# A masked-adjacency layer on one core: the bias as one row, the weight matrix on the loads' queue, two blocks of edge weights moved from ScalarE to VectorE

## The chip, the cores and the metric

The kernel runs on one core of a Trainium2 chip, as one launch. Its time is device microseconds for the launch, and a kernel's time is the median of its runs. The profiled execution is one more run, whose engines and DMA queues were recorded; its span runs from the first to the last recorded instruction of the program and is a little shorter than its device time.

## The reference

The inputs are `x` (4096 x 64), `adj` (4096 x 4096, f32, zeros and ones), a 64 x 64 weight and a bias of 64.

```python
h = jnp.maximum(_layernorm(x, axis=-1), 0.0)
support = h @ weight
mask = (adj != 0).astype(support.dtype)
rank = jnp.cumsum(mask, axis=1)
deg = rank[:, -1:]
k = jnp.minimum(deg, 100.0)
pos = rank - (deg - k)
w = mask * jnp.where(pos > 0, 0.5 ** (k - pos), 0.0)
out = x + w @ support + bias
```

So each row of `adj` gives an edge at a set column the weight one half to the power of the number of set columns behind it, and columns with a hundred or more set ones behind them get nothing. The 64 MB of `adj` are read once; everything else is small.

## The kernel before

The rows are cut into 32 tiles of 128, and each tile is a 2 MB read. The task `load(n)` brings a tile in one transfer, or tiles 0, 1, 28 and 29 in two and tiles 30 and 31 in three. Four tile buffers (`NA`) go round: a load waits until the tile four before it has been read out of its buffer.

A tile then goes through a line of tasks, each on one engine. `convert` (VectorE, L544) turns the f32 tile into mask bytes, four of the eight column pieces per instruction. `flip` (VectorE, L554) transposes it in 32 x 32 blocks. `totals` (TensorE, L562), `split` (ScalarE, L570) and `suffix` (TensorE, L583) count the set columns behind each place. `clamp` (VectorE, L589) limits the count, with a small correction `excess`. `place` (TensorE, L599 and L603) writes exponents into four PSUM banks, j = 0 to 3. `weigh(n, j, part)` (ScalarE, L617) takes one bank through the exponential and writes a block of weights in `wk`; `PARTS` names tiles whose blocks are cut into several instructions. `aggregate(u, h)` (TensorE, L637) multiplies the weights of a pair of tiles with `hr`, the support. After each group of four tiles, `drain` adds the bias (ScalarE L650 or VectorE L652), `turn_back` (TensorE, L658) and `finish` (VectorE, L664) bring the result into row order and add `x`, and `store` writes it.

Ahead of this stands the setup. `fetch` (L339) brings `x` in two halves; `turn`, `center`, `square`, `spread` on TensorE and ScalarE make the layer norm. `support(n)` (TensorE, L512, four groups) multiplies the result with `w2`, which holds the weight matrix twice on its diagonal blocks. `scale(n)` (VectorE, L515) applies the norm's root, and `first` (ScalarE, L522) and `second` (VectorE, L525) split the support into the two parts of `hr`. The correction `excess` comes from `count` (TensorE, L529) and `counted` (VectorE, L532). `warm` (L467) puts spare matmuls on TensorE where the plan sees it idle.

The order on each engine is laid down when the program is built: `plan` takes the tasks one after the other, by their needs, by assumed durations and by the tuned due times in `DUE`, and the engines run them in that order. SyncE issues the loads, the fetches, `load_rest` and the stores in the planned order on one queue. Before, the weight's two transfers are issued by ScalarE on its own queue, at L360, ahead of everything else there. `load_rest` brings the bias into `bias_sb`, one value to a partition (64 elements of 4 bytes in two transfers, L347).

There is a way of making a block of weights on VectorE in the code, which no tile uses: for a pair (tile, j) in `QUICK`, `encode` (L624) turns the exponents into the bits of a float and `take` (L628) scales them into `wk`, in place of `weigh`.

Of the kernel before, what the change touches and what calls it, by code (L numbers as in the profile page):

```python
# [8 lines left out]
F32 = mybir.dt.float32  # L9
# [8 lines left out]
ALU = mybir.AluOpType  # L18
# [18 lines left out]
PIECES = LOADS  # L37
UNITS = [(t, h0, h1) for t in TILES for h0, h1 in (HALVES if t in HALF_UNITS else ((0, 8),))]

PARTS = {31: ((0, 4), (4, 6), (6, 8))}  # L40
QUICK = set()
DRAINS = [(g, 0, 4, g < 6) for g in range(7)] + [(7, 0, 2, False), (7, 2, 4, True)]
STORES = [(0, 0, 16), (1, 0, 12), (1, 12, 14), (1, 14, 16)]
NA, NM, NT, NW, NV, NB = 4, 4, 4, 2, 5, 2

DUE = {
    "fetch": [-6573, -7310],
    "load": [-5992, -6683, -5596, -6079, -7169, -9667, -9541, -11493, -10919, -11290, -11530, -11235, -10266, -10315,
    -11211, -10957, -10678, -11366, -12321, -13820, -14131, -14798, -15615, -14819, -13978, -13919, -13846, -13027,
    -13593, -14902, -7667, -6694, -6587, -6826, -7245, -7519, -6878, -3159, 1510, 1620],  # L50
    "load_rest": [-344],
    "constants": [-454, 600],
    "order_of": [-456],
    "stack": [-625],
    "turn": [-172, 214, 16, 393, 528, 858, 499, 332],
    "turned": [1435, 859, 693, 1141, 1083, 537, 293, 544],
    "center": [171, -98, -659, -200],
    "square": [465, 438, 248, 1102],
    "relu": [1137, 791, 1387, 1058],
    "spread": [-15, 13, -661, -370],  # L60
    "support": [21, -60, -416, -201],
    "scale": [-210, 55, -42, 94],
    "root": [1695],
    "power": [262],
    "count": [530],
    "counted": [543],
    "first": [-860, -667, 302, 408],
    "second": [-75, 111, -482, -354],
    "convert": [-384, -581, 457, 322, -121, -884, 963, 534, -34, -1077, 787, 1056, 108, -349, 764, 1004, 101, -704, 979,
    1309, 707, -163, 1369, 1105, 584, 389, 925, 815, 565, 524, 1124, 802, 750, 45, 1343, 901, 420, 492, 1332, 749, 610,  # L70
    333, 1547, 1282, 1005, 482, 1549, 1648, 364, 550, 1413, 1518, 264, 195, -2196, 1220, 1067, 223, 2066, 2141, -755,
    469, 1297, 60, 1670, 2032],
    "flip": [-564, -432, -860, -830, -320, -589, 240, -276, 665, 258, -130, -71, -67, 442, -190, 483, 174, 848, 950,
    856, 1062, 326, 1060, 1245, 1617, 444, 1652, 901, 1412, 474, 1484, 1416, 1678, 1523, 1720, 1723, 1966, 1776, 2138,
    1090],
    "totals": [615, 533, 701, 950, 1159, 658, 942, 1158, 1268, 370, 1091, 793, 1042, 571, 1431, 749, 1321, -201, 952,
    -123, 771, 524, 719, 698, 807, 1068, 901, 954, 1308, 1166, -194, 861],
    "split": [645, -612, 977, 535, 538, 291, 747, 660, 1196, 965, 1319, 1075, 778, 1018, 734, 1262, 1360, 1594, 1519,
    1656, 1385, 1551, 1729, 1073, 1530, 1511, 1247, 1740, 1524, 2582, -853, -74],
    "suffix": [446, -15, -61, -786, 763, -236, 795, -313, 93, -188, 459, 552, 669, 835, 216, 631, 395, 564, 584, 950,  # L80
    672, 1258, 1076, 1183, 627, 1332, 531, 1082, 731, 1768, 1451, 1290],
    "clamp": [90, 357, 63, 429, -223, 517, 200, 1181, 126, 1287, 489, 1021, 423, 1392, 1268, 1349, 1153, 1062, 714,
    1190, 873, 1239, 869, 899, 504, 1578, -309, -1871, 1035, -1395, 1481, 1978],
    "place": [-1043, -999, -185, 32, -515, -449, -256, -109, -246, 699, -474, 58, -329, -577, -226, 20, -85, 232, -531,
    862, 244, 461, 334, 493, 422, 197, -375, -4620, -3255, -4102, -4101, -13758],
    "weigh": [124, 602, 275, 1009, 635, 1298, 1060, 979, 251, 1028, 726, 1335, 205, 1247, 1050, 936, 591, 779, 700,
    1681, 194, 1357, 1572, 1538, 896, 884, 250, 1348, 553, 1355, 731, 1523, 431, 1605, 947, 1785, 604, 1354, 180, 929,
    381, 2058, 362, 1907, 1129, 801, 383, 1150, 582, 2063, 1301, 2112, 752, 1610, 506, 1510, 659, 2136, 1339, 1936,
    1101, 1819, 669, 1804, 1010, 1979, 967, 1974, 1005, 1542, 510, 2083, 822, 1632, 648, 2361, 1289, 2144, 1196, 1898,
    733, 2030, 647, 2806, 833, 2056, 893, 1515, 249, 1745, 1172, 2639, 1558, 1904, 878, 2400, 992, 2310, 857, 2878,  # L90
    2393, 2725, 1566, 1672, 772, 2619, 1366, 3218, -1655, 2443, -1184, 2580, -535, 2589, 1767, 2743, 78, 2081, 468,
    2913, -3989, 2783, -4899, 2547, -5001, 3060, 2146, -4693, 1918, 2884, 1281, 2811, 2340, 2930, 1917, 2959],
    "aggregate": [334, -267, 593, 289, 1191, 1307, 964, 874, 634, -145, 1348, -270, 752, 1012, -6, 1122, 727, 337, 806,
    -760, 1172, 1394, 515, 867, 914, 74, 936, -373, 1753, 2069, 346, 1555, 388, -82, 1324, 248, 1341, 843, 1279, 1957,
    864, 854, 630, 886, 1416, 1688, 1445, 1564, 1277, 701, 781, 607, 1776, 1685, 1033, 1943, 1694, 873, 660, 1016, 1406,
    1009, 1086, 2299, 1563, 543, 1077, 1566, 1268, 1601, 1408, 2689, 1367, 1074, 1372, 1672, 1796, 1257, 1627, 2498,
    1552, 1370, 1423, 1005, 2226, 1650, 1563, 1956, 2147, 1545, 1525, 1823, 1923, 1908, 2041, 2335, 1453, 1178, 1529,
    2289, 2123, 1291, 1467, 2761, 1965, 1183, 2006, 1763, 2046, 1812, 1619, 2707, 2251, 1680, 1492, 2718, 1786, 1494,
    1802, 3130, -4938, 2631, 2110, 3528, 12, 1317, 1118, -4615],
    "drain": [66, -394, 53, 500, 1525, 818, 356, 1592, -14523],  # L100
    "turn_back": [225, 460, 1136, 1049, 1175, 2364, 545, 1770, -12563],
    "finish": [564, 45, 886, 1501, 2162, 1424, 2379, 1937, -13193],
    "store": [2230, 2470, 2247, -14086],
}
WAIT = 250, 60, 150, 60, 0
PE, DVE, ACT, POOL, SP = range(5)
# [7 lines left out]
def last_of(n, j):  # L114

    return ("encode", n, j) if (n, j) in QUICK else ("weigh", n, j, len(PARTS.get(n, (0,))) - 1)


def tasks():
# [4 lines left out]
    def task(f, args, engine, due, hold, lag, needs, pool=None):  # L124
        if f in DUE:
            due = DUE[f][sum(k[0] == f for k in found)] / 10
        found[f, *args] = f, args, engine, due, hold, lag, needs, pool
# [3 lines left out]
        task("fetch", (r,), SP, 0.5, 0, 0, [])  # L131
    for n, (t, _, _) in enumerate(LOADS):
        task("load", (n,), SP, n, 0, 0, [("convert", m, i) for m, (pt, h0, h1) in enumerate(PIECES) if pt == t - NA for i in range((h1 - h0 + 3) // 4)])
    task("load_rest", (), SP, 4, 0, 0, [("load", 2)])
    task("constants", (0,), DVE, 0, 600, 700, [])
    task("constants", (1,), POOL, 6, 3200, 3300, [("constants", 0)])
    task("order_of", (), DVE, 1, 2950, 3050, [("constants", 0)])
# [9 lines left out]
    for n in range(4):  # L147
        task("spread", (n,), PE, 2, 850, 1050, [("square", n)])
    for n in range(4):
        task("support", (n,), PE, 15, 890, 1090, [("relu", n)], ("v", ("scale", n)))  # L150
        task("scale", (n,), DVE, 10, 610, 730, [("support", n), ("power",)])
    task("root", (), DVE, 3, 480, 600, [("spread", 3)])
    task("power", (), DVE, 3, 1950, 2010, [("root",)])
    task("count", (), PE, 14, 180, 360, [("order_of",)], ("v", ("counted",)))
    task("counted", (), DVE, 14, 160, 250, [("count",)])
    for i in (0, 2, 1, 3):
        task("first", (i,), ACT, 15, 520, 650, [("scale", i % 2 * 2 + 1)])
        task("second", (i,), DVE, 15, 610, 740, [("first", i)])
# [1 line left out]
    for n, (t, h0, h1) in enumerate(PIECES):  # L160
        k = h1 - h0
        lands = [("load", m) for m, (lt, l0, l1) in enumerate(LOADS) if lt == t and l0 < h1 and h0 < l1]
        count = (k + 3) // 4
# [5 lines left out]
    for n, (t, h0, h1) in enumerate(UNITS):  # L169
        second = n > of_tile[t][0]  # L170
        due, size = when[t] + 3 + second, h1 - h0
        parts = PARTS.get(n, ((h0, h1),))
        lands = [("flip", m) for m, (lt, l0, l1) in enumerate(PIECES) if lt == t and l0 < h1 and h0 < l1]
# [6 lines left out]
        for part, (p0, p1) in enumerate(parts):  # L180
            count = (p1 - p0) * 128
# [101 lines left out]
def kernel(  # L283
# [12 lines left out]
    nc = tc.nc  # L296
    P = 128
    N, D = x.shape
    B = N // P
    E = 4  # L300
    H = 2
# [8 lines left out]
    setup = ctx.enter_context(tc.tile_pool(name="setup", bufs=1))  # L310
# [29 lines left out]

    w2 = setup.tile([P, H, D], F32, name="w2")
    bias_sb = const.tile([P, 1], F32, name="bias_sb")

    def load_rest():
        b = bias.rearrange("(d o) -> d o", o=1)
        for d0, d1 in ((0, 8), (8, D)):
            nc.sync.dma_start(bias_sb[d0:d1], b[d0:d1])  # L347

    ones = setup.tile([P, H], F32, name="ones")
    less = setup.tile([P, H, D], F32, name="less")  # L350
# [5 lines left out]
    nc.vector.memset(ones, 0.0)  # L356
    for h in range(H):
        nc.vector.memset(ones[h * D:(h + 1) * D, h:h + 1], 1.0)
    for h in range(H):
        nc.scalar.dma_start(w2[h * D:(h + 1) * D, h, :], weight)  # L360
    pi = setup.tile([P, 6], I32, name="pi")
    nc.gpsimd.iota(pi[:, 0:1], pattern=[[0, 1]], base=0, channel_multiplier=1)
    bits = setup.tile([P, 5], I32, name="bits")
# [8 lines left out]
    excess = const.tile([P, 1], F32, name="excess")  # L372
# [4 lines left out]
    ident = const.tile([P, P], F32, name="ident")  # L377
# [30 lines left out]
    one = setup.tile([P, 1], F32, name="one")  # L408
# [60 lines left out]
    pxs, ns = {}, {}  # L469
# [57 lines left out]
    def count():  # L527
        pxs["count"] = ps_v.tile([P, W], F32, tag="v", name="pn")
        nc.tensor.matmul(pxs["count"][:, :1], near, over, start=True, stop=True)  # L529

    def counted():
        nc.vector.tensor_scalar(excess, pxs.pop("count")[:, :1], one, None, op0=ALU.add)  # L532

    def half():
        return ps_t.tile([P, V], F32, tag="t", name="sums")
# [177 lines left out]
```

## Time and profile before

| | |
|---|---|
| median of 3 runs | 187.79 us (186.71 to 188.05) |
| profiled execution, device time | 188.47 us |
| its span | 186.5 us |
| TensorE, busy | 167.0 us (90%) |
| ScalarE, busy | 152.9 us (82%) |
| VectorE, busy | 151.8 us (81%) |
| DMA of the loads' queue | 69.21 MB, 88.4% of 16 engines' span |
| HBM read | 68.19 MB |

The busy shares are means over the whole span. The loads run until some 20 us before the end, the three engines start late and end late, so the shares of a stage have to be read from that stage. Where a view names a wait, it says which engine or transfer ended it; a wait for several things is put down to the last.

### The profile page before, as it was taken

What the parts mean: (1) busy time and instruction counts of PE and PEld (TensorE: products, weight loads), DVE (VectorE), ACT (ScalarE), POOL (GpSimd) and SP (SyncE); (2) the same over time, 40 slices, a digit from 0 to 9 for tenths busy, and PEclk for the clock granted to TensorE, in tenths of its full rate; (3) what the DMA queues carried; (4) which work ended last, traced back from release to release, by engine and by line L of the source; (5) the groups of instructions that cost most, each with busy time, mean ns of one, the idle gap of its engine ahead of it and who ended that gap; (6) DMA issues with size and microseconds to landing.
All of it is one profiled execution on the core that took longest, in us unless ns stands there. A gap on an engine that the chain in (4) does not pass through costs nothing.

```text
span 186.5 us, 4785 instructions
## 1 busy us (share of the span) xinstructions
PE 167.0 (90%) x2083; PEld 131.2 (70%) x2083; DVE 151.8 (81%) x197; ACT 152.9 (82%) x196; POOL 6.8 (4%) x43
## 2 busy tenths in 40 slices
PE   7999988689979988798999989998899989898982
PEld 5949975467757666676777778675677758686881
DVE  6288799999989898899998889988897989996110
ACT  2664046999999979879999999799949899999951
POOL 7700000000000000000000000000000000000000
PEclk9998599999999999999999999999789999999999
DMA  6999998999999999999999999999999999950200
GB/s 220 383 427 446 418 438 362 425 432 422 436 425 423 432 418 436 422 422 432 432 415 432 422 432 422 425 432 425 429 418 423 411 420 409 416 215 0 90 14 14
DMA packets 6891, 69.55 MB, mean 373 GB/s; under 512 B 982, under 2 KB 1238, under 8 KB 2262
## 3 DMA queue, kind: packets, MB, share of 16 engines
q1 hardware_dynamic: 6710, 69.21, 88.4%
q8 instruction: 16, 0.26, 0.6%
q10 hardware_dynamic: 160, 0.03, 0.1%
q14 instruction: 5, 0.04, 0.1%
HBM read 68.19 MB, written 1.05 MB: 371 GB/s over the span
## 4 chain that ended last, share of the span: by engine, by line
DMA 36%; PE 31%; DVE 16%; ACT 13%; issue 2%
DMA a_sb<-in_adj_dram 36%; PE acc L637 11%; DVE m L544 11%; ACT wk L617 10%; PE pp L512 3%; PE sums L583 2%; PE sums L658 2%; PE none L494 2%; PE v L603 2%; PE pc L482 2%; PE none L467 2%; PE v L599 2%; ACT wk L478 2%; DVE hr L525 1%; ACT sums L570 1%
## 5 line engine op out<-in xcount | busy, mean ns | idle before, releaser
L617 ACT ACTIVATE wk<-v 128x1024 fp32r<-128x1024 uint8 (+2 forms) x136 | 124.3, 1016 | 7.5 <-PE v L603 6.7
L544 DVE TENSOR_SCALAR m<-a_sb 128x2048 uint8<-128x2048 f32 (+1 forms) x66 | 86.4, 1359 | 10.9 <-DMA a_sb<-in_adj_dram 10.9
L637 PE MATMUL acc<-wk,hr 128*128 128x256 f32 x512 | 75.8, 292 | 1.0 <-DVE acc_part L652 0.7
L637 PEld LDWEIGHTS acc<-wk,hr 128*128 128x128 f32 x512 | 64.8, 191 | 8.7 <-issue 5.7
L554 DVE STREAM_TRANSPOSE mt<-m 128x1024 f32<-128x1024 f32 (+2 forms) x40 | 40.8, 1029 | 0.4
L570 ACT ACTIVATE sums<-sums 128x512 f16<-128x512 uint8 x32 | 19.9, 626 | 11.1 <-PE sums L562 10.5
L599 PE MATMUL v<-behind,where 32*128 32x256 f16 x256 | 15.2, 273 | 8.7 <-DVE behind L589 4.6
L589 DVE TENSOR_SCALAR behind<-sums,excess 128x256 f16<-128x256 f32 x32 | 15.2, 477 | 5.7 <-PE sums L583 5.7
L583 PEld LDWEIGHTS <-far 128*128 128x128 f16 x224 | 17.7, 99 | 0.9
L583 PE MATMUL sums<-sums,far 128*128 128x224 f16 (+6 forms) x224 | 18.1, 222 | 0.0
L599 PEld LDWEIGHTS <-where 32*128 32x128 f16 x256 | 5.3, 92 | 15.6 <-issue 13.0
L562 PE MATMUL sums<-mt,band 128*32 128x256 f16 x256 | 13.0, 281 | 1.7 <-DVE mt L554 1.6
L603 PE MATMUL v<-mt,tri 32*32 32x512 f16 x512 | 14.2, 397 | 0.0
L467 PE MATMUL none<-junk 128*128 128x256 bf16 x70 | 10.1, 306 | 1.2 <-DVE junk L353 1.2
L583 PE MATMUL sums<-sums,near 128*128 128x256 f16 x32 | 9.1, 284 | 2.4 <-ACT sums L570 2.2
L467 PEld LDWEIGHTS <-junk 128*128 128x128 bf16 x90 | 8.9, 106 | 3.1 <-DVE junk L353 1.2
L603 PEld LDWEIGHTS <-tri 32*32 32x32 f16 x512 | 4.4, 87 | 6.6 <-issue 6.6
L664 DVE TENSOR_TENSOR xr<-sums,xr 128x256 f32<-128x256 f32 (+1 forms) x9 | 3.5, 386 | 6.8 <-PE sums L658 6.8
L583 PE MATMUL sums<-sums,rest 128*128 128x256 f16 x32 | 8.8, 277 | 0.0
L562 PEld LDWEIGHTS <-band 128*32 128x32 f16 x256 | 4.0, 94 | 6.5 <-DVE mt L554 2.5
L658 PE MATMUL sums<-both,acc_sb 128*128 128x64 f32 x56 | 7.6, 279 | 0.6 <-ACT acc_sb L650 0.6
L658 PEld LDWEIGHTS sums<-both,acc_sb 128*128 128x128 f32 x56 | 6.8, 191 | 1.4 <-ACT acc_sb L650 0.7
(91 smaller groups left out, 86.5 us busy)
## 6 DMA issues: line engine op xcount, KB each, us to landing
a_sb<-in_adj_dram SPq DMA_DIRECT2D x26, 2048.0 KB, 16.9
a_sb<-in_adj_dram SPq DMA_DIRECT2D x10, 1024.0 KB, 14.3
a_sb<-in_adj_dram SPq DMA_DIRECT2D x4, 512.0 KB, 15.2
xr<-in_x_dram SPq DMA_DIRECT2D x2, 512.0 KB, 3.4
out_dram<-xr SPq DMA_DIRECT2D x1, 512.0 KB, 13.7
out_dram<-xr SPq DMA_DIRECT2D x1, 384.0 KB, 2.7
out_dram<-xr SPq DMA_DIRECT2D x2, 64.0 KB, 1.6
w<-in_L_gnn_weight_dram ACTq DMA_DIRECT2D x2, 16.0 KB, 5.6
```

The lines of the kernel that those rows point to most:

```text
L467: nc.tensor.matmul(idle[0][:, idle[1]:idle[1] + 2 * P], junk[:, :P], junk, start=not accs, stop=not accs, skip_group_check=True)
L544: nc.vector.tensor_scalar(words[n][:, k0 * P:k1 * P, :].rearrange("p (h q) e -> p h e q", q=P), tiles[t][:, (h0 + k0) * W:(h0 + k1) * W].r ...
L554: nc.vector.transpose(to[:, h0:h1], m_v.rearrange("p (h c l) -> p h c l", c=4, l=SUB))
L562: nc.tensor.matmul(tot[SUB * c:SUB * (c + 1), r], band[:, SUB - 12 - 4 * a:2 * SUB - 12 - 4 * a], masks[t][:, c, r, a], start=(a == 0), st ...
L570: nc.scalar.activation(sums8[t][:, :, r], pts.pop((n, "n")).bitcast(U8).rearrange("p (i f) -> p f i", f=4)[:, :2, r], AF.Copy, bias=-136.0)
L583: nc.tensor.matmul(o, l, m, start=(k == 0), stop=(k == len(todo) - 1), skip_group_check=True)
L589: nc.vector.tensor_scalar(behind[n][:, r], pts.pop((n, "s"))[:, r], excess, float(MAX_NEIGH), op0=ALU.subtract, op1=ALU.min)
L599: nc.tensor.matmul(vs[n, j][:, h0:h1, a, :], where[q, a, :], behind[n][q, r], start=(a == 0), stop=False, skip_group_check=True)
L603: nc.tensor.matmul(vs[n, j][SUB * c:SUB * (c + 1), h0:h1], tri[q, q], masks[t][q, c, r, :].rearrange("p (h r) a -> p h a r", r=SUB), start ...
L617: nc.scalar.activation(to[:, :, :, j, :], v[:, :2, x], AF.Exp, scale=-LN2, bias=-38.0 * LN2)
L637: nc.tensor.matmul(accs[g][:, at:at + 2 * P], hr[:, h * 4 + e, :, :].rearrange("p s d -> p (s d)"), wts[u][:, s, 2 * h + a].rearrange("p i ...
L658: nc.tensor.matmul(pts["o", d][:, k, :], sums[d][:, k * P:(k + 1) * P], both, start=True, stop=True)
```

## The change

Five things differ.

1. The bias comes in one transfer as a row of 64 values into `bias_row`. `count` gets a TensorE transpose of that row into a second column of its PSUM tile, and `counted` a copy from there into `bias_sb`.
2. The two transfers of the weight move from ScalarE's queue into `load_rest`, so to SyncE's queue, behind the bias row. In `tasks`, `load_rest` now needs `fetch(1)`, and `support` and `count` are entered as needing `load(3)`, the second half of tile 1.
3. `PARTS` cuts the weight blocks of tile 29 into two each.
4. `QUICK` names block 3 of tiles 30 and 31, which `encode` and `take` now make on VectorE.
5. All due times in `DUE` are other ones, and `count` and `counted` are entered with longer durations, so the planned order on the engines differs in many places.

The short description that goes with the change also names a late drain on VectorE. The table of drains is the same in both kernels: the drains of group 6 and of the first half of group 7 are on VectorE in both.

```diff
-PARTS = {31: ((0, 4), (4, 6), (6, 8))}
-QUICK = set()
+PARTS = {29: ((0, 4), (4, 8)), 31: ((0, 4), (4, 6), (6, 8))}
+QUICK = {(30, 3), (31, 3)}
 DRAINS = [(g, 0, 4, g < 6) for g in range(7)] + [(7, 0, 2, False), (7, 2, 4, True)]
...
-    task("load_rest", (), SP, 4, 0, 0, [("load", 2)])
+    task("load_rest", (), SP, 3.5, 0, 0, [("fetch", 1)])
...
-        task("support", (n,), PE, 15, 890, 1090, [("relu", n)], ("v", ("scale", n)))
+        task("support", (n,), PE, 15, 890, 1090, [("relu", n), ("load", 3)], ("v", ("scale", n)))
...
-    task("count", (), PE, 14, 180, 360, [("order_of",)], ("v", ("counted",)))
-    task("counted", (), DVE, 14, 160, 250, [("count",)])
+    task("count", (), PE, 14, 300, 480, [("order_of",), ("load", 3)], ("v", ("counted",)))
+    task("counted", (), DVE, 14, 320, 410, [("count",)])
...
+    bias_row = setup.tile([1, D], F32, name="bias_row")
 
     def load_rest():
-        b = bias.rearrange("(d o) -> d o", o=1)
-        for d0, d1 in ((0, 8), (8, D)):
-            nc.sync.dma_start(bias_sb[d0:d1], b[d0:d1])
+        nc.sync.dma_start(bias_row, bias.rearrange("(o d) -> o d", o=1))
+        for h in range(H):
+            nc.sync.dma_start(w2[h * D:(h + 1) * D, h, :], weight)
...
-    for h in range(H):
-        nc.scalar.dma_start(w2[h * D:(h + 1) * D, h, :], weight)
...
+        nc.tensor.transpose(pxs["count"][:D, 1:2], bias_row, ident[:1, :1])
 
     def counted():
-        nc.vector.tensor_scalar(excess, pxs.pop("count")[:, :1], one, None, op0=ALU.add)
+        nc.vector.tensor_scalar(excess, pxs["count"][:, :1], one, None, op0=ALU.add)
+        nc.vector.tensor_copy(bias_sb[:D], pxs.pop("count")[:D, 1:2])
```

In the built program SyncE's queue begins, before, with both halves of `x`, loads 0 to 5 (tiles 0 to 3), load 6 (tile 4) and the bias. After, it begins with the first half of `x`, load 0, the second half of `x`, loads 1 to 5, the bias row, the two weight transfers, and then load 6. So the weight stands behind tile 3 on that queue, while the plan counts it as there with load 3, the end of tile 1. The first `support` matmul waits for the two weight transfers, as before. VectorE's order from there on is: first `scale`, both converts of tile 2, second `scale`, its flip, two `second`, third `scale`, `counted` with the bias copy, fourth `scale`, the first two `clamp`. On ScalarE all four `first` now stand ahead of the first `weigh`.

## The prediction

> **What bounds the kernel now.** I read the page first (busy shares, slices, the chain's sums, the groups), then the chain in order of time, the loads' queue, and ScalarE's timeline. The page's slices, engine rows and DMA row, and its chain summed by engine:
>
> ```profile
> DVE  6288799999989898899998889988897989996110
> ACT  2664046999999979879999999799949899999951
> PEclk9998599999999999999999999999789999999999
> DMA  6999998999999999999999999999999999950200
> DMA 36%; PE 31%; DVE 16%; ACT 13%; issue 2%
> ```
>
> Each digit is 4.66 us. The loads are busy to slice 35 (some 166 us), and no engine is idle in between: DMA has the largest share of the chain, not all of it. In order of time (start, length, what):
>
> ```profile
> 17.91 5.34 PE pp L512 x24
> ...
> 23.28 0.69 DVE wk L515
> ...
> 36.64 16.58 DMA a_sb<-in_adj_dram
> ...
> 158.25 3.77 ACT wk L617 x4
> ```
>
> There are three stretches. Up to 33 us the setup is the path, with `support` (L512) in it. From 36.6 to 127.6 the chain keeps returning to loads, for 16 to 18 us each time; between the landings at 107.98 and 127.55 that end two of these pieces lie four tiles, 4.89 us for 2 MB. After 127.6 no load is in it, and the chain passes between TensorE, ScalarE and VectorE: they are behind the loads and run at their own pace. So a late start of the setup is paid back only where engines now wait for data, and not after 127.6.
>
> **Part 1, the weight on the loads' queue.** This decides. The queue's own issues, and landing times from two views (the page's DMA issues; then the loads' line, fastest, median and slowest):
>
> ```profile
> 5.59 0.33 SPq L336 DMA_DIRECT2D a_sb<-in_adj_dram  x1
> ...
> out_dram<-xr SPq DMA_DIRECT2D x1, 512.0 KB, 13.7
> out_dram<-xr SPq DMA_DIRECT2D x2, 64.0 KB, 1.6
> w<-in_L_gnn_weight_dram ACTq DMA_DIRECT2D x2, 16.0 KB, 5.6
> ...
> DMA to landing us min/median/max: 9.9/16.6/22.1
> ```
>
> The store of 512 KB is issued while loads are still queued and lands after 13.7 us; the small stores, behind nothing, take 1.6. So what stands behind loads on this queue waits for them. The weight now comes through ScalarE's queue, past the loads, in 5.6 us. In the changed program loads 4 and 5 (tiles 2 and 3) are issued ahead of it, although the plan counts it as there with tile 1: neither has a wait in front of it. Load 5 is the one issued at 5.59, and it is the 22.1: the load before it, issued from 4.16, is already being converted at 23.89, and load 6, issued at 13.46, is converted at 34.0, less than 22.1 later. So load 5 lands at 5.59 + 22.1 = 27.7, and the weight rows and bias row behind it at some 27.9 (0.2 for 32 KB in short rows, an estimate between nothing and the 1.6 of a 64 KB store). The reversed order of `x`'s second half and load 0 delays the layer norm by half a tile's time, 2.4 us; its end at 17.9 becomes some 20, hidden below 27.9. SyncE's own new waits, for the first half of `x` and load 0, end before load 6 may be issued (13.46, held by the conversion of tile 0).
>
> From there by the changed order. `support` took 6.7 us for four groups, 1.7 a group, at a granted clock of 0.51 (windows view, 17 to 24). First `scale` at 27.9 + 1.7 = 29.6. VectorE then has, by the spacing of starts in 23 to 31: four `scale` 2.4, a pair of converts 2.6, two `second` 1.2, a flip 1.2, `counted` and the new copy 0.4 (0.22 each, the row of L532), two `clamp` 0.8: 8.6, done at 38.2. Before, the second `clamp` ended at 30.3. VectorE is 7.9 late. TensorE has four groups of support (6.7), two `totals` (0.64 at full clock, 1.3 at half), the two small matmuls (0.4) and a `suffix` (0.6): it reaches 36.9, so VectorE and it arrive together. In the row below, the first `weigh` came 1.2 after the end of the first `clamp` (28.76); that clamp now ends at 37.8, so the first `weigh` starts at 39.0. ScalarE is 9.0 late. Were the clock full by then, the first group would take half, 0.85, and all would be some 1 us earlier; I keep the measured half, and 1 us for the near end.
>
> ```profile
> 29.93 1.01 ACT L617 ACTIVATE wk<-v 128x1024 fp32r<-128x1024 uint8 x1
> ...
> 47.69 1.94 ACT L617 ACTIVATE wk<-v 128x1024 fp32r<-128x1024 uint8 x2 [0.24 <-PE v L603]
> ...
> 138.33 1.03 ACT L617 ACTIVATE wk<-v 128x1024 fp32r<-128x1024 uint8 x1 [2.41 <-PE v L603]
> ```
>
> What of the 9.0 is paid back? Counting four blocks a tile, these rows are the first blocks of tiles 0, 4 and 23. From 0 to 23 the kernel took 108.4 us, 4.71 a tile, with VectorE waiting 8.0 us for loads between 36 and 128. With a backlog it needs less: 4.44 a tile over tiles 0 to 4, and 4.59 over tiles 23 to 30 (138.33 to 170.5), where it also is behind the loads. So 23 tiles pay back 23 x (4.71 - 4.59) = 2.8 to 23 x (4.71 - 4.44) = 6.2; I take the middle, 4.5, because the fast row has no drains yet and the slow one has the split last tiles. From tile 23 on both kernels are behind the loads and nothing more is paid back. 9.0 - 4.5 = **+4.5 us**. VectorE's 7.9 against its 8.0 of waits sets no tighter bound. Could the loads themselves fall dry? Load 9 waits for tile 3's conversion, before at 30.9 to 34.1; that is now behind the second `clamp` and ends at about 42, when the stream has reached the end of load 8 (27.7 + 3 x 4.89 = 42.4). A dry spell of 0 to 1.5 us there falls into a time when VectorE has a backlog: nothing, and 1.5 for the far end.
>
> Two rules of the Trainium skill bear on this part. Its page "Trainium Kernel Development and Optimization", section Key Constraints, says that DMAs from SyncE, ScalarE and GpSimd run on the same engines and interleave, and that issuing from several saves only issue time. By that the move would cost 1.2 us of issue on SyncE and no delay of `support`, and the sum would be that of the first rival below; the 13.7 of the store against the 1.6 of its neighbours speaks against using it so. The page "TensorE: Matmul & The Clock Gate", section What's actually happening, says that TensorE falls to half its clock after one idle window of about 3.4 us and needs a busy one to come back. TensorE would stand idle from about 20 to 27.9, so by the page `support` starts at half clock; the trace shows half clock at this place only for a TensorE that was busy with short matmuls. By the page the sum stands as it is; by the opposite case it would be the 1 us less named above.
>
> **Part 2, the bias as a row.** Before, 64 values of 4 bytes go through behind load 6. Between 28 and 33 us the loads ran at 367 GB/s against 426 after, 0.7 us of stream lost; I put that down to them. One row instead gains up to 0.7 where loads bind. With the engines behind the loads throughout, it gains nothing; 0 to 0.7, I take 0. The transpose and copy (0.2 each) are in the sum above. `drain` needs the bias 25 us later. ScalarE loses two issues of 1.18 us at 1.36 to 2.54, where it has nothing to do before 5.73: nothing.
>
> **Part 3, the late blocks.** ScalarE has no gap over 0.31 us from 158 to 179.6:
>
> ```profile
> 172.32 7.24 ACT L617 ACTIVATE wk<-v 128x1024 fp32r<-128x1024 uint8 x15
> ```
>
> It loses one whole block (starts 0.91 apart) and one in three parts (0.50, 0.26, 0.26): 1.9. Tile 29 in halves costs eight times 0.48 instead of four times 0.91: 0.2 more. Net 1.7 less on the path. VectorE gets two `encode` and four `take`; no such row exists. Nearest by size: 0.78 (a convert of 128x1024) to 1.40 (128x2048) for an `encode`; 0.7 per 128x512 for a `take`, so 2.8 for two whole blocks: 4.4 to 5.6 in all. After 169.9 VectorE waited 0.99, 1.65 and 3.27 between its rows, 5.9 in all; that covers it, if the blocks fall into those gaps, but then a block on VectorE and not ScalarE is last before the closing `aggregate`. Between a gain of 1.7 and a loss of 1.0 (an uncovered `take`), I take a gain of **0.8**.
>
> **Sum.** 188.47 + 4.5 - 0.8 = 192.2 for an execution like the profiled one, which lies 0.7 above the median: **191.5**. Its own range: 9.0 - 6.2 - 1.7 = +1.1, and 1 less at full clock, to 9.0 - 2.8 + 1.5 + 1.0 = +8.7; so 187.9 to 196.5.
>
> **The rivals.** *First, the other side: the weight does not wait.* If its rows pass the queued loads as they do on ScalarE's queue, they are there 5.6 after an issue at some 9 (load 0 was landed at 9.5 before), at 15. Up to 20 (when the layer norm is through) that costs nothing; beyond it, each microsecond counts. Then the late start is 2 us and is paid back, the bias gives 0.7, the tail 0.8: 186.3. For it: the change's plan counts on it, and the landing of the bias before is not shown. Against: the store. 0.12.
>
> *Second, all is paid back.* If the whole stretch runs at 4.44 a tile, 2.8 stay; half a clock window less in 133 to 137 (granted 0.57 there, with ScalarE's 2.41 wait behind it), which a busier TensorE may not have, takes 1.8, and the tail 0.8: 188.0. For it: 8.0 us of VectorE's waits. Against: TensorE is 90% busy and has no such slack. 0.20.
>
> *Third, nothing is paid back,* because TensorE paces every tile: +9.0, less the tail, 196.0. Against: the 4.44 of the first tiles. 0.12. The forecast keeps 0.56.
>
> **The numbers.** 1% of the median, 1.9 us, is what a measurement here can tell from no change: faster is below 185.9, slower above 189.7. Faster: a part of the first rival, 0.08. Same: the rest of it, most of the second, the forecast's low end: 0.23. Slower: 0.69. The range leaves out the first rival's better half and the third's worse half: 187.0 to 196.2.
>
> **What would show it.** The first `support` matmul at about 27.9, behind the weight's transfers; the first `weigh` at 39; tile 23's first block some 4 to 5 later than 138.3; VectorE's waits for loads nearly gone; the tail after the last `weigh` unchanged. A `support` at 20 refutes part 1; a `weigh` of tile 23 at 138 refutes the payback.

## The result and the profile after

The changed kernel takes 194.84 us (median of 6 runs, 193.15 to 196.21), against 187.68 for the kernel before: a ratio of 1.0376 with an interval of 1.0324 to 1.0427, so slower by some 7 us. Here and below a time is the median of all runs of a kernel, while a ratio leaves out slow runs, those over 1.5% above the fastest of the same kernel, so the two can differ by some tenths of a per cent and, with four runs, by one. The profiled execution took 194.73 us with a span of 192.7, 6.3 more than the one before. The forecast had 191.5.

The page's slices and its chain by engine, each digit now 4.82 us:

```profile
DVE  7677309999999998889889895799989798998620
ACT  2574003499999999989399899999988999999630
PEclk9999658999999999999999999999999999999998
DMA  5999999949999999999999999999999999710200
PE 32%; ACT 29%; DVE 20%; DMA 13%; issue 4%; SPq 0%; ACTq 0%
```

VectorE has a hole in slices 4 and 5, counted from 0 (19 to 29 us), ScalarE too, and the granted clock dips there. The share of DMA in the chain fell from 36 to 13%, and most of what is left of it is one transfer. The chain in order of time (start, length, what):

```profile
1.70 6.27 DMA xr<-in_x_dram
...
7.98 19.11 DMA w<-in_L_gnn_weight_dram
27.09 0.14 issue
27.23 2.06 PE pp L513 x8
29.28 0.02 issue
29.31 0.69 DVE wk L516
...
36.76 0.90 DVE behind L592 x2
```

By the chain, the second weight transfer is issued only when the second half of `x` has landed, at 7.98, and is then under way for 19.1 us. TensorE starts `support` right behind it. The page's DMA issues give its median beside the stores, and the TensorE timeline the wait:

```profile
out_dram<-xr SPq DMA_DIRECT2D x1, 512.0 KB, 13.7
...
out_dram<-xr SPq DMA_DIRECT2D x2, 64.0 KB, 1.7
w<-in_L_gnn_weight_dram SPq DMA_DIRECT2D x2, 16.0 KB, 19.6
```

```profile
27.23 3.59 PE L513 MATMUL pp<-w,wk 128*128 128x128 f32 x16 [8.79 <-DMA w<-in_L_gnn_weight_dram]
30.74 0.65 PE L565 MATMUL sums<-mt,band 128*32 128x256 f16 x16
31.32 2.05 PE L513 MATMUL pp<-w,wk 128*128 128x128 f32 x16
```

So a transfer of 16 KB in 64 rows takes 19.6 us on this queue (median of the two), where it took 5.6 on ScalarE's. The same 16 matmuls cost 3.59 us and, 4 us later, 2.05. ScalarE's rows that answer to those of before, the first blocks of tiles 0 and 23 (the third row holds tile 23's four blocks and the first of tile 24):

```profile
38.19 3.77 ACT L620 ACTIVATE wk<-v 128x1024 fp32r<-128x1024 uint8 x4
...
145.03 0.60 ACT L573 ACTIVATE sums<-sums 128x512 f16<-128x512 uint8 x1 [1.05 <-PE sums L565]
145.71 4.83 ACT L620 ACTIVATE wk<-v 128x1024 fp32r<-128x1024 uint8 x5
```

38.2 against 29.9, and 145.7 against 138.3: 8.3 us late at tile 0 and 7.4 late at tile 23. VectorE's longest waits between 36 and 165 us (total, times, longest one) no longer name a load:

```profile
DVE behind L592 <- PE sums L586: 10.1, 13, 2.4
...
ACT wk L620 <- PE v L606: 5.9, 7, 3.3
```

Before, the same view of the same stretch had both:

```profile
DVE m L544 <- DMA a_sb<-in_adj_dram: 8.6, 14, 1.4
...
DVE behind L589 <- PE sums L583: 4.1, 9, 1.0
```

VectorE's idle time did not go, it changed its name. That is the open point the experiments had to settle: why so little was paid back.

### The profile page after: what moved, and what is told of

Same layout as the page of the kernel before. It is cut to its first block, busy times and chain, and to the rows that moved or that the text cites. A ratio compares the mean times of both kernels' runs of the same rounds, so it can differ in the third digit from the quotient of the medians.

```text
span 192.7 us, 4786 instructions
## 1 busy us (share of the span) xinstructions
PE 164.8 (85%) x2078; PEld 127.8 (66%) x2078; DVE 154.2 (80%) x204; ACT 150.2 (78%) x196; POOL 7.8 (4%) x43
## 4 chain that ended last, share of the span: by engine, by line
PE 32%; ACT 29%; DVE 20%; DMA 13%; issue 4%; SPq 0%; ACTq 0%
ACT wk L620 23%; PE acc L640 18%; DVE m L547 11%; DMA w<-in_L_gnn_weight_dram 10%; DVE mt L557 5%; ACT sums L573 4%; DMA xr<-in_x_dram 3%; PE sums L661 3%; PE v L606 3%; PE sums L586 3%; PE v L602 3%; PE sums L565 2%; DVE behind L592 2%; ACT acc_sb L653 1%; DVE hr L526 1%
## 5 line engine op out<-in xcount | busy, mean ns | idle before, releaser
L620 ACT ACTIVATE wk<-v 128x1024 fp32r<-128x1024 uint8 (+2 forms) x136 | 122.3, 996 | 8.0 <-PE v L606 7.5
L640 PE MATMUL acc<-wk,hr 128*128 128x256 f32 x512 | 73.1, 289 | 3.4 <-ACT wk L620 1.7
L640 PEld LDWEIGHTS acc<-wk,hr 128*128 128x128 f32 x512 | 63.5, 188 | 10.5 <-ACT wk L620 4.2
L592 DVE TENSOR_SCALAR behind<-sums,excess 128x256 f16<-128x256 f32 x32 | 15.6, 490 | 10.5 <-PE sums L586 10.1
L602 PE MATMUL v<-behind,where 32*128 32x256 f16 x256 | 16.5, 273 | 5.2 <-ACT wk L620 3.4
L513 PE MATMUL pp<-w,wk 128*128 128x128 f32 x32 | 5.6, 349 | 8.8 <-DMA w<-in_L_gnn_weight_dram 8.8
L513 PEld LDWEIGHTS pp<-w,wk 128*128 128x128 f32 x32 | 5.3, 259 | 9.1 <-issue 9.1
L468 PE MATMUL none<-junk 128*128 128x256 bf16 x63 | 9.5, 310 | 1.2 <-DVE junk L356 1.2
L468 PEld LDWEIGHTS <-junk 128*128 128x128 bf16 x84 | 8.3, 107 | 3.4 <-DVE junk L356 1.2
L516 DVE TENSOR_TENSOR wk<-pp,y 128x512 f32<-128x512 f32 x4 | 2.8, 712 | 8.2 <-PE pp L513 8.2
## 6 DMA issues: line engine op xcount, KB each, us to landing
a_sb<-in_adj_dram SPq DMA_DIRECT2D x10, 1024.0 KB, 11.4
w<-in_L_gnn_weight_dram SPq DMA_DIRECT2D x2, 16.0 KB, 19.6
```

The source lines that it names most:

```text
L468: nc.tensor.matmul(idle[0][:, idle[1]:idle[1] + 2 * P], junk[:, :P], junk, start=not accs, stop=not accs, skip_group_check=True)
L513: nc.tensor.matmul(pp[:, b, :, :], rx[:, (4 * n + b) * P:(4 * n + b + 1) * P], w2.rearrange("p h d -> p (h d)"), start=True, stop=True)
L592: nc.vector.tensor_scalar(behind[n][:, r], pts.pop((n, "s"))[:, r], excess, float(MAX_NEIGH), op0=ALU.subtract, op1=ALU.min)
L602: nc.tensor.matmul(vs[n, j][:, h0:h1, a, :], where[q, a, :], behind[n][q, r], start=(a == 0), stop=False, skip_group_check=True)
L620: nc.scalar.activation(to[:, :, :, j, :], v[:, :2, x], AF.Exp, scale=-LN2, bias=-38.0 * LN2)
L640: nc.tensor.matmul(accs[g][:, at:at + 2 * P], hr[:, h * 4 + e, :, :].rearrange("p s d -> p (s d)"), wts[u][:, s, 2 * h + a].rearrange("p i ...
```

## The experiments

The theory: the weight's place in the queue makes the start late, and nearly all of that reaches the end. The rivals: the new order of tasks or the late blocks are slow by themselves; short rows on the loads' queue cost something wherever they stand; a late start should be paid back, and something else eats it.

**The weight back on ScalarE's queue** (the changed kernel otherwise).

```diff
+    for h in range(H):
+        nc.scalar.dma_start(w2[h * D:(h + 1) * D, h, :], weight)
...
         nc.sync.dma_start(bias_row, bias.rearrange("(o d) -> o d", o=1))
-        for h in range(H):
-            nc.sync.dma_start(w2[h * D:(h + 1) * D, h, :], weight)
```

> The changed kernel with the two weight transfers back on ScalarE's queue; the bias row stays behind tile 3, and everything else stays as changed. Theory (the weight's place in the queue makes the start late): first support matmul at 18 to 20 us, where its operands are ready; the correction count still waits for the bias row at 27, so the first weigh comes at 30 to 31, against 38.2; time 186.5 to 189. Rival (the new order and the late blocks make the kernel slower, the start is only part): the start is early in the same way, but the time stays at 191 or more.

Measured: 187.64 us, ratio to the kernel before 1.0007 (0.9970 to 1.0044). `support` starts at 18.7, the first `weigh` at 30.5:

```profile
29.27 1.16 ACT L523 ACTIVATE hr<-wk 128x512 fp32r<-128x512 f32 x2 [2.57 <-DVE wk L516]
30.54 3.77 ACT L620 ACTIVATE wk<-v 128x1024 fp32r<-128x1024 uint8 x4
```

The whole loss goes with two lines. The new order, the late blocks and the bias row are all still in this kernel.

**The weight where the plan counts it**, on the loads' queue behind tile 1.

```diff
+        if (f, args) == ("load", (4,)):
+            load_rest()
-        does[f](*args)
+        if f != "load_rest":
+            does[f](*args)
```

> The changed kernel with bias row and weight issued right behind load 3 (tile 1), where the plan counts them, ahead of loads 4 and 5. Theory: they land at about 16, the first support at 18 to 20, the first weigh at 30 to 31, time 186 to 188.5, the same as with the weight on ScalarE's queue or a little less. Rival (transfers of short rows on the loads' queue cost by themselves, wherever they stand): the stream loses a microsecond or more there and the time lies above 189. Rival (order and late blocks): 191 or more.

Measured: 187.83 us, ratio 1.0002 (0.9971 to 1.0033); the weight takes 11.4 us and lands at 15.9, the first `weigh` starts at 30.3. So neither the queue nor short rows on it are the fault; what stands ahead of them is.

**The weight alone late, in the kernel before.**

```diff
-    for h in range(H):
-        nc.scalar.dma_start(w2[h * D:(h + 1) * D, h, :], weight)
...
+        if (f, args) == ("load", (5,)):
+            for h in range(H):
+                nc.sync.dma_start(w2[h * D:(h + 1) * D, h, :], weight)
```

> The kernel before, in its own order and with its own bias and blocks; only the two weight transfers are put on the loads' queue behind load 5 (tile 3). Theory: first support at 27.2, first weigh at 38, and the time 192 to 195.5, so the larger part of the change's loss by this edit alone. Rival (the payback was small in the changed kernel because of its new order: ScalarE lost 3.3 us ahead of tile 12 there): the start is as late, but the older order pays back 4 us or more, and the time is 189 to 191.5.

Measured: 192.77 us, ratio 1.0244 (1.0173 to 1.0316). This one edit makes 5.4 of the 7.2 us by the medians, and 4.6 (3.2 to 5.9) of 7.1 by the ratios. The first `weigh` is at 38.7, 8.8 late, so 3.4 were paid back in the old order by the medians, 4.2 (2.9 to 5.6) by the ratio. The wait view from 36 to 165 us has no load either:

```profile
DVE behind L587 <- PE sums L581: 8.1, 13, 1.1
```

**One tile further back**, behind load 6, in the changed kernel.

```diff
+        if f != "load_rest":
+            does[f](*args)
+        if (f, args) == ("load", (6,)):
+            load_rest()
```

> The changed kernel with bias row and weight one tile further back, behind load 6 (tile 4). Theory (late start, little of it paid back): the weight lands 4.9 us later, at 32, the first weigh at 43, and the time is 4 to 5 us above the changed kernel, 198.5 to 200. Rival (payback grows with the backlog, the rest of the loss has another cause): 195 to 197.

Measured: 200.37 us, a little above the range, ratio 1.0651 (1.0577 to 1.0726). The weight lands at 30.7, the first `weigh` is at 41.7, 3.5 us after the changed kernel's, and the time 5.5 above it: more than the start, with 3.4 us of half clock (a granted clock of 0.50) from 85.9 on in the profiled run. A larger backlog brought no more payback.

**One tile less far back**, behind load 4 (tile 2): in the kernel before, the weight alone, and in the changed kernel, bias row and weight. Each is one number away from an earlier run (the weight alone late; the weight where the plan counts it).

```diff
-        if (f, args) == ("load", (5,)):
+        if (f, args) == ("load", (4,)):
```

```diff
-        if (f, args) == ("load", (4,)):
+        if (f, args) == ("load", (5,)):
```

> The kernel before with the weight alone on the loads' queue behind load 4 (tile 2), one tile less far back than in the run that put it behind tile 3. The weight lands at about 21.3, the first support 3.5 us later than before, the first weigh at 33 to 33.5. That other run paid back 3.4 of 8.8 us. If the older order holds a fixed slack of 3 us or so: no loss or up to 0.6 us, 187.2 to 188.1. If a share of the delay is paid back: 188.7 to 189.9. If nothing: 190.5 to 191.2.

> The changed kernel with bias row and weight behind load 4 (tile 2). They land at about 21, the first support 2.3 to 2.6 us after the 18.5 to 18.7 of the early runs of this order, the first weigh at 32.5 to 33. If the changed order pays nothing back: 189.8 to 190.5. If it has a fixed slack, too: 187.5 to 188.5.

Measured: in the old order 187.70 us, ratio 1.0015 (0.9982 to 1.0048), with the first `weigh` at 33.1, 3.2 late; in the changed order 189.34 us, ratio 1.0127 (1.0082 to 1.0172), with the first `weigh` at 31.8, 1.3 after the run with the weight on ScalarE's queue, and the time 1.7 above that run's. A fixed slack of some 3 us fits the old order: by the ratios it swallowed 2.9 of 3.2 (the interval includes all of it) and 4.2 of 8.8, by the medians 2.8 and 3.4. A fixed share does not fit: the 39 to 48% of the later start would leave 1.7 to 2.0 of the 3.2, and the interval ends at 0.9. The changed order shows no slack. Waits of VectorE between 36 and 165 us, of the first of these two runs:

```profile
DVE m L542 <- DMA a_sb<-in_adj_dram: 5.5, 8, 1.2
```

Put together, from the traces (us; `weigh` is the first one, `place` the end of the last one, waits those of VectorE from 36 to 165):

| order | weight | weigh | place | between | waits for loads | for suffix |
|---|---|---|---|---|---|---|
| old | ScalarE's queue (kernel before) | 29.9 | 175.2 | 145.3 | 8.6 | 4.1 |
| old | behind tile 2 | 33.1 | 174.6 | 141.5 | 5.5 | 3.5 |
| old | behind tile 3 | 38.7 | 179.4 | 140.7 | none | 8.1 |
| new | ScalarE's queue | 30.5 | 174.0 | 143.5 | 9.1 | 2.5 |
| new | behind tile 2 | 31.8 | 175.5 | 143.6 | 1.1 | 9.3 |
| new | behind tile 3 (changed kernel) | 38.2 | 181.4 | 143.2 | none | 10.1 |

The first row's profiled run has 3.4 us of half clock in it (133 to 137), the fifth row's too (93.8 to 97.3). In these three rows of the new order the length between is the same within 0.4 us, whether VectorE waits 9.1 us for loads or not at all. Three more runs of the new order (their edits stand above and below): 143.0 with the late blocks back on ScalarE; 144.7 with the weight behind tile 4 and 3.4 us of half clock; 146.0 with the weight behind tile 1 and 6.8 us of half clock. The line for the loads in the first row of the new order, which the changed kernel's view does not have:

```profile
DVE m L547 <- DMA a_sb<-in_adj_dram: 9.1, 15, 2.2
```

One place shows how: ScalarE's wait ahead of tile 12's first block, first in the run with the weight on its own queue, then in the changed kernel.

```profile
87.26 2.86 ACT L620 ACTIVATE wk<-v 128x1024 fp32r<-128x1024 uint8 x3 [3.27 <-PE v L606]
```

```profile
94.61 2.86 ACT L620 ACTIVATE wk<-v 128x1024 fp32r<-128x1024 uint8 x3 [3.27 <-PE v L606]
```

3.27 us in both, 7.3 us apart, although VectorE waits for loads around it in the first run and for none in the second. In the changed kernel's TensorE timeline the tile's `suffix` (91.46) stands behind eight `aggregate` matmuls that wait 0.86 us for a block of ScalarE's, and in the other run (84.11) behind the same eight with the same wait. The pause belongs to the order. Between the first `weigh` and the last `place`, 143.2 us in the changed kernel, TensorE is busy for 130.4, ScalarE for 133.3 and VectorE for 127.3: no engine is full, and which of them, or which chain of waits between them, sets the length was not tried.

**The plan told of the late weight.** The changed kernel, with the needs corrected to the place where the weight really stands; the due times stay.

```diff
-[("relu", n), ("load", 3)]
+[("relu", n), ("load", 5)]
...
-[("order_of",), ("load", 3)]
+[("order_of",), ("load", 5)]
```

> The changed kernel with the weight where it is, but support and count entered in the plan as needing load 5 (tile 3), so that the order is laid down for the late start. Theory (the order holds pauses laid for an early weight, as ahead of tile 12, and repeats them when it starts late): the first weigh still at 37.5 to 39, and 1.5 to 4 us paid back, 191 to 193.5. Rival (from the first weigh on the engines need some 154 us in any order): 194 to 196.

Measured: 194.27 us as the median of four runs from 190.95 to 195.16, ratio 1.0267 (1.0151 to 1.0382). The interval, some 190 to 194.5 us, reaches into both cases. The profiled run, at 195.00, has the first `weigh` at 36.8 and the last `place` ending at 181.3, so 144.5 between, with 3.4 us of half clock. Whether an order laid down for the late start, with due times tuned for it, would pay more back stays open.

**The bias row alone**, in the kernel before, issued behind the two halves of `x`.

```diff
-        b = bias.rearrange("(d o) -> d o", o=1)
-        for d0, d1 in ((0, 8), (8, D)):
-            nc.sync.dma_start(bias_sb[d0:d1], b[d0:d1])
+        nc.sync.dma_start(bias_row, bias.rearrange("(o d) -> o d", o=1))
```

> The kernel before with the bias alone as a row, issued right behind the two halves of x, with the transpose and the copy; weight, blocks and order as before. Forecast of the study: the loads run at 425 GB/s or more between 28 and 33 us, against 367, and 0.7 us of stream is won; since the engines are behind the loads at the end, the time falls by 0 to 0.7, to 186.7 to 187.4. Rival (the loads set the end): 1 us or more less, below 186.4. Rival (the short rows were not the cause of the dip): the rate there stays below 400.

Measured: 187.16 us, ratio 0.9995 (0.9954 to 1.0036). The windows view from 28 to 33 us (busy times, then clock, DMA share and GB/s), before and with the row:

```profile
28.00:33.00 5.00, 4.14 (x58) 2.52 (x56) 5.00 (x9) 3.61 (x5) 0.00 (x0) 1.00 0.90 367
```

```profile
28.00:33.00 5.00, 3.78 (x55) 2.18 (x53) 5.00 (x9) 3.72 (x5) 0.00 (x0) 1.00 1.01 429
```

The dip is gone with the row, 0.7 us of stream are won, and the time does not move. That the short rows alone make the dip is not shown, though. They stand at the same place, behind load 6, in the run below with the late blocks moved in the kernel before, and there the same stretch has none:

```profile
28.00:33.00 5.00, 5.00 (x69) 2.85 (x66) 5.00 (x8) 4.74 (x7) 0.00 (x0) 0.66 1.01 420
```

The run with an earlier first block has them too and runs at 423 GB/s; the two runs of the old order with a late weight dip, to 361 and 380. So short rows come with a dip in three profiled runs of five, and no run without them falls below 413.

**The late blocks alone**: in the kernel before, they go to VectorE; in the changed kernel, back to ScalarE.

```diff
+        if f == "weigh" and args[0] in (30, 31) and args[1] == 3:
+            if args[2] == 0:
+                encode(args[0], 3)
+                for part in range(len(PARTS.get(args[0], (0,)))):
+                    take(args[0], 3, part)
+        else:
+            does[f](*args)
```

```diff
+        if f == "take":
+            weigh(*args)
+        elif f != "encode":
+            does[f](*args)
```

> The kernel before with block 3 of tiles 30 and 31 made by encode and take on VectorE, all else as before. Forecast of the study: ScalarE is on the path there, so 0.8 to 1.9 us are won, 185.5 to 186.6. Rival (behind the last place TensorE has 48 aggregate matmuls of some 0.13 us, and they set the end): the same time as before within 0.5, with the last place to the end as long as before.

> The changed kernel with block 3 of tiles 30 and 31 back on ScalarE, tile 29 still in halves. Forecast of the study: 0.8 to 1.9 us more than the changed kernel, 195.6 to 196.7. Rival (TensorE's last matmuls set the end): the changed kernel's time within 0.6, 194.2 to 195.4.

Measured: 187.95 us, ratio 1.0049 (1.0017 to 1.0081), and 195.00 us, ratio 1.0386 (1.0308 to 1.0464) against the changed kernel's 194.84 and 1.0376. Nothing is won by them in either; in the kernel before, the interval even says a loss of 0.3 to 1.5 us. TensorE behind the last `place`, in the changed kernel and in the one with the blocks back on ScalarE:

```profile
181.31 2.81 PE L640 MATMUL acc<-wk,hr 128*128 128x256 f32 x20
184.69 1.63 PE L640 MATMUL acc<-wk,hr 128*128 128x256 f32 x12 [0.58 <-DVE acc_part L655]
186.16 0.55 PE L661 MATMUL sums<-both,acc_part 128*128 128x64 f32 x4
186.52 2.13 PE L640 MATMUL acc<-wk,hr 128*128 128x256 f32 x16
```

```profile
179.74 2.08 PE L640 MATMUL acc<-wk,hr 128*128 128x256 f32 x16
182.02 0.74 PE L640 MATMUL acc<-wk,hr 128*128 128x256 f32 x4 [0.20 <-ACT wk L620]
183.34 1.69 PE L640 MATMUL acc<-wk,hr 128*128 128x256 f32 x12 [0.58 <-DVE acc_part L655]
184.86 0.55 PE L661 MATMUL sums<-both,acc_part 128*128 128x64 f32 x4
185.22 2.13 PE L640 MATMUL acc<-wk,hr 128*128 128x256 f32 x16
```

48 matmuls in both, over 7.3 and 7.6 us, nearly back to back. From the end of the last `place` to the end of the span it is 11.37 us in the changed kernel and 11.65 with the blocks on ScalarE; 11.30 in the kernel before and 11.87 with its late blocks on VectorE.

**An earlier first block**, in the kernel before: first `clamp`, `place` and `weigh` ahead of their neighbours, no spare matmuls ahead of that `place`.

```diff
+        warm(0 if (f, args) == ("place", (0,)) else spare)
+        if (f, args) == ("second", (0,)):
+            clamp(0)
+        if (f, args) == ("first", (1,)):
+            place(0)
+            weigh(0, 0)
+        if (f, args) not in (("clamp", (0,)), ("place", (0,)), ("weigh", (0, 0, 0))):
+            does[f](*args)
```

> The kernel before with the first clamp moved ahead of one second and the flip of tile 2, no spare matmuls ahead of the first place, and the first weigh ahead of two of the first: the first weigh starts at about 28.2 against 29.9, the sums of work are the same but for 16 spare matmuls. If the length from the first weigh to the last place is fixed by the order, 0.8 to 1.7 us are won: 185.7 to 186.6. If only one block comes early and the line behind it is held by the same VectorE work, nothing is won: 187 to 188.

Measured: 187.46 us, ratio 1.0003 (0.9968 to 1.0038). The first `weigh` comes at 27.3, 2.6 early, but tile 4's at 48.1, 0.4 late, so one early block did not move the line behind it. The profiled run has half clock from 24.4 to 31.3 and from 38.1 to 41.5, which may have held tile 4 too; the time shows no gain either way. No version tried is faster than the kernel before by more than its interval.

## Why the prediction was right, and where its size was off

**The weight's place: right.** Forecast landing of load 5 at 27.7 and `support` at 27.9; measured 26.7 and 27.2. The rival on the other side, in which the rows pass the queued loads, fell with the 19.6 us. The page "Trainium Kernel Development and Optimization", section Key Constraints, by which issuing from several engines saves only issue time, is contradicted for this use: 5.6 and 6.0 us on ScalarE's queue, 19.6 on SyncE's behind 9 MB, and 7 us of device time between the two.

**The late start: right, 9.0 forecast and 8.3 measured.** The weight landed at 27.1 and `support` began 0.7 earlier than forecast; the first group took 2.1 us in place of 1.7, and from the first `scale` to the first `weigh` it was 8.9 in place of 9.4, most of it VectorE's rows back to back (29.31 to the two `clamp` at 36.76). The clock, for which I had named 1 us, moved none of this as far as the chain shows: of `support` only the first group is in the chain, and it ran at half clock throughout. The windows view of the changed kernel has the clock, in the column ahead of the last two:

```profile
17.00:24.00 7.00, 1.44 (x13) 1.35 (x13) 2.84 (x13) 0.48 (x1) 0.00 (x0) 0.73 1.02 433
24.00:28.00 4.00, 0.77 (x4) 0.80 (x4) 0.00 (x0) 0.00 (x0) 0.00 (x0) 0.50 1.00 410
28.00:33.00 5.00, 5.00 (x45) 4.63 (x45) 3.69 (x4) 1.09 (x2) 0.00 (x0) 0.75 1.00 426
```

It halves at 20.3 and is whole again at 30.5, 3.3 us after `support` began; I had kept the half for all of it. Of the rule of the page "TensorE: Matmul & The Clock Gate", section What's actually happening (half clock after an idle window of some 3.4 us, full after a busy one), the return agrees with these rows. The fall fits less well: TensorE's last matmuls ahead of the wait end at 18.4, 1.9 us before it, and they were short ones.

**The payback: this term failed.** I had put 4.5 of the 9.0 as paid back, from a pace of 4.44 to 4.59 us a tile with a backlog against 4.71, and held VectorE's 8.0 us of waits for loads to be room for it. The sign that I had named for it, tile 23's first block 4 to 5 us late, came out as 7.4. Against the same order with an early start (30.5 to the last `place` at 174.0), the changed kernel pays back 0.3 of 7.7 us, and by the medians 0.5 (187.64 to 194.84). The old order pays back 3 us or so in both runs that start it late. VectorE's waits for loads were not slack of the kernel: once the loads were early, VectorE waited as long for TensorE (10.1 us for `suffix`, against 2.5 with the early start), which works in an order laid down when the program is built. The pace of tiles 0 to 4 was a pace of that stretch of the order, not what the rest can do: with a backlog throughout, the changed kernel took 4.67 us a tile from tile 0 to 23 (38.19 to 145.71), and 4.69 with the early start (30.54 to 138.33). So for this term the third rival, in which nothing is paid back, was right, and I had given it 0.12 against 0.56; its 196.0 lies 1.2 from the median, my 191.5 lies 3.3 from it. Its reason, that TensorE paces every tile, is not shown.

**The loads running dry: right that it costs nothing, its length too small.** Loads 8, 9 and 10 land at 41.4, 48.9 and 54.5, spacings of 7.5 and 5.6 against 4.9, so 3.3 us of stream are lost where I had 0 to 1.5; VectorE waits for none of these loads.

**The bias: right in its price**, 0 us, with the 0.7 of stream won as worked out; that the short rows always cost it is contradicted by the two runs that have them without a dip.

**The tail: the term was mis-sized.** I took a gain of 0.8 between a gain of 1.7 and a loss of 1.0; it is 0 within the noise in the changed kernel and a loss of 0.9 (0.3 to 1.5) in the kernel before. ScalarE had no gaps there, but TensorE had 48 `aggregate` matmuls behind the last `place`, and the end follows them. Of the new instructions an `encode` took 1.23 us (0.78 to 1.40 forecast) and a whole `take` 0.68 (1.4).

With 8.3 in place of 9.0, 2.1 in place of 4.5 (6.2 are left at the last `place`, against the profiled execution before with its half clock) and a loss of 0.1 in place of the gain of 0.8, the sum is the 6.3 us that the two profiled executions differ by; the three terms are read at the first `weigh`, the last `place` and the end, so they add up by construction. The chance of slower was well placed, because the largest term was right; the middle was 3.3 us low, by the payback and the tail, and that the start was put 0.7 too late made up a little of it by luck.

## What to carry to other kernels

Here a transfer of 16 KB landed behind all that was issued on its queue before it: at 15.9 us behind 5 MB, 27.1 behind 9 MB, 30.7 behind 11 MB. So its time is read from the program's order and the bytes ahead of it, not from what a plan says it needs. A small urgent transfer goes on another queue or ahead of the large ones; both gave the time back here, while telling the plan of the late weight did not clearly do so. An engine's waits for data are not by themselves room to make up a late start: shifting the start by two different amounts shows how much room an order really has, 3 us in one of these and none in the other, where the waits alone said 8 to 9. An engine without gaps near the end is not yet the one that the end waits for: count what is left to do behind the last step that everything needs.

## What the hardware showed unexpectedly

The granted clock drops to half for pieces of 3.4 us and multiples in the middle of a run, at places that differ between near equal kernels: 133 to 137 in the profile before; 75.3 to 78.7 and 95.8 to 99.2 in the run with the weight behind tile 1, whose profiled execution took 189.75 us against its median of 187.83; 74.2 to 81.1 in the run with the bias row alone. The work per tile there is the same as ahead of it. What sets them off was not tried.
